# A graph transformer layer and a graph attention layer: context and layer 1 in another form, and the TensorE order laid down by hand

## The chip, the cores and the metric

The kernel runs on one core of a Trainium2 chip. The metric is the device time of one execution in microseconds; four to eight executions are taken of each kernel, and they agree within 0.3%. PE is TensorE, PEld its weight loads, DVE is VectorE, ACT is ScalarE and POOL is GpSimd in the lines of the profile. The "chain that ended last" is the chain of work followed back from the last instruction, at each step to what released it.

## The reference

There are 128 graphs ("batches") of 128 nodes with 512 features each, all in f32, and a weighted adjacency `adj` of 128x128 for each of them.

```python
# layer 0: pre-norm transformer, 8 heads of 64
h = relu(layernorm(x))
q, k, v = h @ Wq.T + bq, h @ Wk.T + bk, h @ Wv.T + bv      # split in heads
attn = softmax((q @ k.T) / 8 * (adj + adj))                # over the keys
x = x + (attn @ v) @ Wo.T + bo
# layer 1: graph attention
h = relu(layernorm(x))
Wh = h @ W
e = leaky_relu(Wh @ a[:512] + (Wh @ a[512:]).T, 0.2)
attention = softmax(where(adj > 0.5, e, -9e15), axis=1)    # over the rows
x = x + elu(attention @ Wh)
```

## The kernel before

Batches go in groups of four: the 512 rows of a group are the moving columns of the q and k projections. A framework writes the program: its scheduler decides the order of the instructions of each engine, from the order of the code and its own estimates. The parts that the change touches:

```python
def normed_T(dst, src, mv, rstd, b):
    """relu(layernorm(src)) with the features on the partitions."""
    hn = work.tile([P, E], F32, name="hn")
    nc.vector.tensor_scalar(hn, src, mv[:, b, 0:1], rstd[:, b : b + 1], op0=OP.subtract, op1=OP.mult)
    pt = ps1.tile([P, C, P], F32, name="pt", tag="ps1")
    for c in range(C):
        nc.tensor.transpose(pt[:, c, :], hn[:, c * P : (c + 1) * P], ident)
    nc.scalar.activation(dst, pt, AF.Relu)

def layer0_output(g, b, v, at, rs):
    # ... at is transposed into aT, head by head
    for j in range(H):
        head = 2 * (j % C) + j // C
        nc.tensor.matmul(pc[:, head, :], aT[:, j, :], v[:, head * D : (head + 1) * D], start=True, stop=True)
    nc.vector.tensor_tensor(cx, pc, rs[:, :, None].to_broadcast([P, H, D]), OP.mult)
    for c in range(C):
        nc.tensor.transpose(pt[:, c, :], cxf[:, c * P : (c + 1) * P], ident)
    nc.scalar.copy(cxT, pt)
    po = rows_matmul(cxT, wo_sb)
    # ... residual, statistics

def layer1_rows(g, b):
    normed_T(h2T, xs[g][:, b, :], mv1s[g], rstd, b)      # four transposes
    pw = rows_matmul(h2T, w1_sb)                         # project first, attend later
    # ...

# main loop, shortened
for g in range(NG + 1):
    layer0_qk(g)
    for b in range(G):
        scored = layer0_scores(g, b)
        if pending:
            layer0_output(*pending)
        pending = scored
        # ... layer 1 of group g - 1, the norm of group g + 1
```

## Time and profile before

| | before |
|---|---|
| time, median | 3728.24 us (3725.69 to 3730.71, four runs) |
| TensorE busy, share of the span | 90% |
| TensorE's share of the chain that ended last | 83% |
| mean granted TensorE clock | 0.964 |
| span per batch | 3721.6 / 128 = 29.07 us |

Four things are needed to read what follows. Each f32 matmul of the code stands in the trace as two matmul instructions, here called passes. In the groups of instructions a row is "line, engine, operation, output<-input, shapes, count | busy us, mean ns of one | idle time of the engine ahead of them and what ended it". TensorE's instructions overlap, so the mean of one is longer than the distance from one to the next: a 128x512 f32 pass reads 595 ns and follows its predecessor after 429 ns (3.43 us for eight). And the granted clock is what the throttle left of TensorE's full speed.

Two views of the kernel before are the group of the hn transposes (hn is the normed rows of a batch) and the timeline of TensorE around a context. The columns of the timeline are start, length, engine, line, operation, and in brackets the idle time before and who ended it.

```profile
L119 PE MATMUL pt<-ident,hn 128*128 128x128 f32 x1024 | 163.2, 278 | 85.0 <-DVE hn L116 85.0
```

```profile
1918.80 0.66 PE L210 MATMUL pt<-ident,cx 128*128 128x128 f32 x4 [0.79 <-DVE cx L206]
1920.13 5.40 PE L141 MATMUL pm<-wo,cxT 128*128 128x512 f32 x8 [0.68 <-ACT cxT L212]
```

TensorE waits for VectorE's scaled copy of the context, transposes it, waits for ScalarE's copy of the transposed context, and only then projects. The eight passes of the projection take 5.40 us here instead of 3.70, because the clock falls meanwhile: it is 1.00 up to 1920.8 and 0.50 from there to 1924.2. The change removes this sequence.

### The profile page before, as it was taken

Reading aid. Unit: us, or ns where it says so; the run is one execution under the profiler, and the core shown is the slowest. Engines: PE = TensorE matmul, PEld = TensorE weight load, DVE = VectorE, ACT = ScalarE, POOL = GpSimd, SP = SyncE. Lnnn points to the kernel's source line nnn. Section 1 sums busy time; section 2 is a strip of 40 time slices with the busy share of each in tenths; the row PEclk is TensorE's granted clock in tenths of the full one; section 3 lists DMA queues with packets and bytes.
Section 4 is the critical chain, followed back from the end, with each engine's and each line's share of the span. In section 5 each row is a group of like instructions: output and inputs, shape, how many; then the busy total and the mean of one; then the engine's idle time right before and its main releaser. Section 6 shows DMA issues by size and latency. Waiting matters only on the chain.

```text
span 3721.6 us, 32428 instructions
## 1 busy us (share of the span) xinstructions
PE 3335.5 (90%) x12416; PEld 1780.7 (48%) x12416; DVE 1620.8 (44%) x3008; ACT 975.1 (26%) x3201; POOL 260.3 (7%) x295
## 2 busy tenths in 40 slices
PE   7999889998889988999989899889998898998996
PEld 4444444454444444444444444444444544444443
DVE  3343443434444345444444443544444444445434
ACT  2222232222332223222223221232222222223221
POOL 1000000000000000000000000000000000000000
PEclk9999999999999999999999999999999999999998
DMA  3000000000000000000000000000000000000000
GB/s 110 1 26 26 26 3 23 26 26 26 4 26 23 26 26 15 15 23 26 26 18 12 23 26 26 26 3 26 23 26 26 4 26 23 26 26 8 18 12 23
DMA packets 55115, 83.87 MB, mean 23 GB/s; under 512 B 2736, under 2 KB 19120, under 8 KB 54960
## 3 DMA queue, kind: packets, MB, share of 16 engines
q1 hardware_dynamic: 50688, 75.50, 5.9%
q10 hardware_dynamic: 4272, 6.30, 0.5%
q8 instruction: 98, 1.61, 0.2%
q14 instruction: 57, 0.47, 0.0%
HBM read 48.24 MB, written 33.55 MB: 22 GB/s over the span
## 4 chain that ended last, share of the span: by engine, by line
PE 83%; DVE 8%; ACT 6%; issue 1%; POOL 1%; DMA 1%; ACTq 0%; POOLq 0%; DVEq 0%
PE pm L141 40%; PE pp L126 24%; PE pc L204 6%; PE sc L177 4%; PE pt L210 2%; DVE cx L206 2%; PE pt L119 2%; DVE at L179 2%; ACT h2T L120 2%; DVE st L110 2%; ACT cxT L212 2%; PE ph L269 1%; PE pa L196 1%; DVE x L214 1%; PE pb L240 1%
## 5 line engine op out<-in xcount | busy, mean ns | idle before, releaser
L141 PE MATMUL pm<-w,h2T 128*128 128x512 f32 x1024 | 525.3, 660 | 74.6 <-ACT h2T L120 74.6
L141 PE MATMUL pm<-wo,cxT 128*128 128x512 f32 x1024 | 524.2, 659 | 67.0 <-ACT cxT L212 67.0
L126 PE MATMUL pp<-hT,wq 128*128 128x512 f32 x1024 | 449.9, 597 | 42.8 <-ACT hT L120 42.8
L141 PE MATMUL pm<-wv,hT 128*128 128x512 f32 x1024 | 463.8, 595 | 0.2
L126 PE MATMUL pp<-hT,wk 128*128 128x512 f32 x1024 | 444.7, 592 | 0.0
L185 ACT ACTIVATE at<-at,nmx 128x128 f32<-128x128 f32 x1024 | 396.6, 389 | 118.3 <-DVE nmx L181 59.2
L141 PEld LDWEIGHTS pm<-w,h2T 128*128 128x128 f32 x1024 | 202.8, 208 | 318.3 <-issue 215.2
L141 PEld LDWEIGHTS pm<-wo,cxT 128*128 128x128 f32 x1024 | 201.5, 207 | 307.7 <-issue 213.7
L170 DVE TENSOR_TENSOR v<-pm,bv 128x512 f32<-128x512 f32 x128 | 88.2, 689 | 583.1 <-PE pm L141 583.1
L214 DVE TENSOR_TENSOR x<-pm,x 128x512 f32<-128x512 f32 x128 | 88.6, 692 | 551.1 <-PE pm L141 551.1
L126 PEld LDWEIGHTS pp<-hT,wq 128*128 128x128 f32 x1024 | 192.7, 191 | 281.3 <-issue 230.7
L126 PEld LDWEIGHTS pp<-hT,wk 128*128 128x128 f32 x1024 | 194.6, 190 | 244.9 <-issue 244.9
L136 ACT ACTIVATE kT<-pp,bk 128x512 f32<-128x512 f32 x128 | 88.0, 687 | 803.0 <-PE pp L126 803.0
L141 PEld LDWEIGHTS pm<-wv,hT 128*128 128x128 f32 x1024 | 187.0, 190 | 206.8 <-issue 199.2
L204 PEld LDWEIGHTS pc<-v,aT 128*128 128x128 f32 x2048 | 249.0, 192 | 54.6 <-issue 45.2
L204 PE MATMUL pc<-v,aT 128*128 128x64 f32 x2048 | 253.5, 274 | 0.8 <-DVE aT L198 0.7
L116 DVE TENSOR_SCALAR hn<-x,mv,rstd 128x512 f32<-128x512 f32 x256 | 136.8, 546 | 263.1 <-PE pt L119 203.9
L177 PE MATMUL sc<-kT,qT 64*128 64x128 f32 x2048 | 223.1, 303 | 18.5 <-DVE at L179 18.5
L119 PE MATMUL pt<-ident,hn 128*128 128x128 f32 x1024 | 163.2, 278 | 85.0 <-DVE hn L116 85.0
L133 DVE TENSOR_SCALAR qT<-pp,bq 128x512 f32<-128x512 f32 x128 | 96.1, 751 | 323.5 <-PE pp L126 323.5
L155 POOL TENSOR_TENSOR x<-x,bo 128x512 f32<-128x512 f32 x128 | 162.0, 1267 | 887.0 <-DVE hn L116 879.9
L119 PEld LDWEIGHTS pt<-ident,hn 128*128 128x128 f32 x1024 | 127.2, 143 | 194.4 <-DVE hn L116 92.2
(52 smaller groups left out, 3039.5 us busy)
## 6 DMA issues: line engine op xcount, KB each, us to landing
x<-in_x SPq DMA_DIRECT2D x32, 1024.0 KB, 5.3
out<-x SPq DMA_DIRECT2D x32, 1024.0 KB, 4.3
adj<-in_adj SPq DMA_DIRECT2D x32, 256.0 KB, 2.8
wq<-in_wqT ACTq DMA_DIRECT2D x1, 1024.0 KB, 8.3
wk<-in_wkT ACTq DMA_DIRECT2D x1, 1024.0 KB, 13.9
wv<-in_wvT ACTq DMA_DIRECT2D x1, 1024.0 KB, 13.2
wo<-in_woT ACTq DMA_DIRECT2D x1, 1024.0 KB, 10.6
w<-in_w ACTq DMA_DIRECT2D x1, 1024.0 KB, 12.5
```

The costliest lines, as they stand in the source:

```text
L116: nc.vector.tensor_scalar(hn, src, mv[:, b, 0:1], rstd[:, b : b + 1], op0=OP.subtract, op1=OP.mult)
L119: nc.tensor.transpose(pt[:, c, :], hn[:, c * P : (c + 1) * P], ident)
L126: nc.tensor.matmul(pp, w[:, c, f * P : (f + 1) * P], hT[:, c].rearrange("p b s -> p (b s)"), start=(c == 0), stop=(c == C - 1),)
L133: nc.vector.tensor_scalar(dst, pp, bq_sb[:, f : f + 1], QSCALE, op0=OP.add, op1=OP.mult)
L136: nc.scalar.activation(dst, pp, AF.Identity, bias=bk_sb[:, f : f + 1])
L141: nc.tensor.matmul(pm, lhsT[:, c, :], w[:, c, :], start=(c == 0), stop=(c == C - 1))
L155: nc.gpsimd.tensor_tensor(xs[g][:, b, :], xs[g][:, b, :], bo_sb, OP.add)
L170: nc.vector.tensor_tensor(v, pv, bv_sb, OP.add)
L177: nc.tensor.matmul(sc[:, s * C + i, :], qT[r, i, cols], kT[r, i, cols], start=True, stop=True)
L185: nc.scalar.activation(at[:, j, :], at[:, j, :], AF.Exp, bias=nmx[:, j : j + 1], accum_out=sums[:, head : head + 1])
L204: nc.tensor.matmul(pc[:, head, :], aT[:, j, :], v[:, head * D : (head + 1) * D], start=True, stop=True)
L214: nc.vector.tensor_tensor(xg[:, b, :], po, xg[:, b, :], OP.add)
```

## The change

The intent, as far as the code shows it, has five parts.

- The context is made already transposed, as v^T x attention^T, two heads side by side in the two halves of the output partitions. Four transposes and one of two copies go. The attention must then be scaled by its row sums ahead of its transpose, and GpSimd does it.
- Layer 1 applies the attention to the normed rows, then projects. Its four transposes go, and so does the transpose of the adjacency, which is loaded transposed.
- Constants are folded (the bias of v into that of the output, the two vectors of layer 1 into W).
- The pipeline is one of single batches: in step t, batch t is scored, t-1 projected, t-2 finished in layer 1, t+8 normed.
- TensorE's order is taken from the code and not from the scheduler.

```diff
+    def context(b):
+        pc = ps1.tile([P, C, S], F32, name="pc", tag="ps1")
+        for i in range(C):
+            for s in range(2):
+                head = 2 * i + s
+                nc.tensor.matmul(
+                    pc[s * D : (s + 1) * D, i, :], vs[b][:, head * D : (head + 1) * D], ats[b][:, s * C + i, :],
+                    start=True, stop=True,
+                )
+        cxs[b] = work.tile([P, C, S], F32, name="cxT")
+        nc.scalar.copy(cxs[b], pc)
...
+    def hidden(b):
+        mv = row_stats(xs[b])
+        rstd = rstd_of(mv)
+        hn = work.tile([P, E], F32, name="hn")
+        nc.vector.tensor_scalar(hn, xs[b], mv[:, 0:1], rstd, op0=OP.subtract, op1=OP.mult)
+        pt = ps1.tile([P, C, P], F32, name="pt", tag="ps1")
+        for c in range(C):
+            nc.tensor.transpose(pt[:, c, :], hn[:, c * P : (c + 1) * P], ident)
+        nc.scalar.activation(hTs[g][:, :, i, :], pt, AF.Relu)
...
+        nc.gpsimd.tensor_tensor(at, at, rs[:, :, None].to_broadcast([P, H, S]), OP.mult)   # in scores(b)
...
+        nc.vector.tensor_scalar(neg, adjTs[b], 0.5, NEG_INF, op0=OP.is_le, op1=OP.mult)    # in output0(b)
...
+    def gather1(b):
+        for c in range(C):
+            nc.tensor.matmul(pg[:, c, :], h2[:, c * P : (c + 1) * P], w, start=True, stop=True)
+        nc.scalar.copy(gT, pg)
...
+    with tc.manual_schedule(engines={PE}):
+        for t in range(B + 3):                       # the guards on t are left out here
+            load_x(t + 2 * G); load_adj(t + 2)
+            scores(t)
+            qk_unit(g + 1, 2 * i)
+            attention1(t - 2)
+            output0(t - 1)
+            hidden(t + 2 * G)
+            values(t)
+            gather1(t - 2)
+            qk_unit(g + 1, 2 * i + 1)
+            attn_T(t)
+            output1(t - 2)
+            context(t)
```

More of the change, by code (lines that the diff above doesn't have):

```diff
@@ L9 @@
 F32 = mybir.dt.float32
-U8 = mybir.dt.uint8
 AF = mybir.ActivationFunctionType
@@ L13 @@
 AX = mybir.AxisListType
+PE = mybir.EngineType.PE
 P = 128
@@ L29 @@
     adj: bass.AP,
+    adjT: bass.AP,
     wqT: bass.AP,
@@ L44, with load_x, load_adj @@
     C = E // P
-    NG = B // G
     QSCALE = 2.0 / D**0.5
     const = ctx.enter_context(tc.tile_pool(name="const", bufs=1))
-    io = ctx.enter_context(tc.tile_pool(name="io", bufs=3))
+    io = ctx.enter_context(tc.tile_pool(name="io", bufs=15))
+    aio = ctx.enter_context(tc.tile_pool(name="aio", bufs=6))
     grp = ctx.enter_context(tc.tile_pool(name="grp", bufs=2))
     work = ctx.enter_context(tc.tile_pool(name="work", bufs=2))
-    small = ctx.enter_context(tc.tile_pool(name="small", bufs=4))
+    small = ctx.enter_context(tc.tile_pool(name="small", bufs=6))
     ps1 = ctx.enter_context(tc.tile_pool(name="ps1", bufs=4, space=bass.MemoryType.PSUM))
     ps2 = ctx.enter_context(tc.tile_pool(name="ps2", bufs=2, space=bass.MemoryType.PSUM))
-    xs, adjs = {}, {}
-    def load(g):
-        rows = slice(g * G, (g + 1) * G)
-        xs[g] = io.tile([P, G, E], F32, name="x")
-        nc.sync.dma_start(xs[g], x[rows].rearrange("b s e -> s b e"))
-        adjs[g] = io.tile([P, G, S], F32, name="adj")
-        nc.sync.dma_start(adjs[g], adj[rows].rearrange("b s t -> s b t"))
-    load(0)
+    xs, adjs, adjTs = {}, {}, {}
+    def load_x(b):
+        xs[b] = io.tile([P, E], F32, name="x")
+        nc.sync.dma_start(xs[b], x[b])
+    def load_adj(b):
+        adjs[b] = aio.tile([P, S], F32, name="adj")
+        nc.sync.dma_start(adjs[b], adj[b])
+        adjTs[b] = aio.tile([P, S], F32, name="adjT")
+        nc.sync.dma_start(adjTs[b], adjT[b])
+    for b in range(2 * G):
+        load_x(b)
     ident = const.tile([P, P], F32, name="ident")
     make_identity(nc, ident)
-    mhalf = const.tile([P, G], F32, name="mhalf")
+    mhalf = const.tile([P, 1], F32, name="mhalf")
     nc.gpsimd.memset(mhalf, -0.5)
@@ L93, with row_stats @@
     wv_sb = weight(wvT, "wv")
-    bv_sb = row(bv, 0, "bv")
     wo_sb = weight(woT, "wo")
-    bo_sb = row(bo, 0, "bo")
+    bv_sb = column(bv, "bv")
+    c_sb = row(bo, 0, "c")
     w1_sb = weight(w1, "w1")
-    as_sb = row(a1, 0, "a_src")
-    at_sb = row(a1, E, "a_dst")
+    us_sb = row(a1, 0, "u_src")
+    ut_sb = row(a1, E, "u_dst")
+    for b in range(2):
+        load_adj(b)
     def rstd_of(mv):
-        r = small.tile([P, G], F32, name="rstd")
-        nc.gpsimd.tensor_scalar_add(r, mv[:, :, 1], EPS)
+        r = small.tile([P, 1], F32, name="rstd")
+        nc.gpsimd.tensor_scalar_add(r, mv[:, 1:2], EPS)
         nc.gpsimd.tensor_tensor(r, r, mhalf, OP.pow)
         return r
-    def row_stats(mv, b, src):
+    def row_stats(src):
         st = small.tile([P, nc.vector.BN_STATS_DIM], F32, name="st")
         nc.vector.bn_stats(st, src)
-        nc.vector.bn_aggr(mv[:, b, :], st)
-    def normed_T(dst, src, mv, rstd, b):
-        hn = work.tile([P, E], F32, name="hn")
-        nc.vector.tensor_scalar(hn, src, mv[:, b, 0:1], rstd[:, b : b + 1], op0=OP.subtract, op1=OP.mult)
-        pt = ps1.tile([P, C, P], F32, name="pt", tag="ps1")
-        for c in range(C):
-            nc.tensor.transpose(pt[:, c, :], hn[:, c * P : (c + 1) * P], ident)
-        nc.scalar.activation(dst, pt, AF.Relu)
-    def project(dst, w, hT, finish):
-        for f in range(C):
-            pp = ps1.tile([P, G * S], F32, name="pp", tag="ps1")
-            for c in range(C):
-                nc.tensor.matmul(
-                    pp, w[:, c, f * P : (f + 1) * P], hT[:, c].rearrange("p b s -> p (b s)"),
-                    start=(c == 0), stop=(c == C - 1),
-                )
-            finish(dst[:, f], pp, f)
-    def finish_q(dst, pp, f):
-        nc.vector.tensor_scalar(dst, pp, bq_sb[:, f : f + 1], QSCALE, op0=OP.add, op1=OP.mult)
-    def finish_k(dst, pp, f):
-        nc.scalar.activation(dst, pp, AF.Identity, bias=bk_sb[:, f : f + 1])
+        mv = small.tile([P, 2], F32, name="mv")
+        nc.vector.bn_aggr(mv, st)
+        return mv
     def rows_matmul(lhsT, w):
@@ L142, in rows_matmul @@
         return pm
-    hTs, qks, mv1s, l1s = {}, {}, {}, {}
-    def layer0_norm(g, b):
-        if b == 0:
-            mv = small.tile([P, G, 2], F32, name="mv")
-            for i in range(G):
-                row_stats(mv, i, xs[g][:, i, :])
-            hTs[g] = grp.tile([P, C, G, S], F32, name="hT"), mv, rstd_of(mv)
-        hT, mv, rstd = hTs[g]
-        normed_T(hT[:, :, b, :], xs[g][:, b, :], mv, rstd, b)
-        nc.gpsimd.tensor_tensor(xs[g][:, b, :], xs[g][:, b, :], bo_sb, OP.add)
-    def layer0_qk(g):
-        hT = hTs[g][0]
-        qT = grp.tile([P, C, G * S], F32, name="qT")
-        kT = grp.tile([P, C, G * S], F32, name="kT")
-        project(qT, wq_sb, hT, finish_q)
-        project(kT, wk_sb, hT, finish_k)
-        qks[g] = qT, kT
@@ L165, in layer0_scores @@
-    def layer0_scores(g, b):
-        ag, hT, (qT, kT) = adjs[g], hTs[g][0], qks[g]
-        cols = slice(b * S, (b + 1) * S)
-        pv = rows_matmul(hT[:, :, b, :], wv_sb)
-        v = work.tile([P, E], F32, name="v")
-        nc.vector.tensor_tensor(v, pv, bv_sb, OP.add)
+    hTs, qks, ats, vs, cxs, l1s = {}, {}, {}, {}, {}, {}
+    def hidden(b):
+        g, i = divmod(b, G)
+        if i == 0:
+            hTs[g] = grp.tile([P, C, G, S], F32, name="hT", bufs=3)
+        mv = row_stats(xs[b])
[6 more added lines that the diff above has]
+        nc.scalar.activation(hTs[g][:, :, i, :], pt, AF.Relu)
@@ new lines, in qk_unit @@
+    def qk_unit(g, n):
+        f, is_k = divmod(n, 2)
+        if n == 0:
+            qks[g] = grp.tile([P, C, G * S], F32, name="qT"), grp.tile([P, C, G * S], F32, name="kT")
+        w = wk_sb if is_k else wq_sb
+        dst = qks[g][is_k][:, f]
+        pp = ps1.tile([P, G * S], F32, name="pp", tag="ps1")
+        for c in range(C):
+            nc.tensor.matmul(
+                pp, w[:, c, f * P : (f + 1) * P], hTs[g][:, c].rearrange("p b s -> p (b s)"),
+                start=(c == 0), stop=(c == C - 1),
+            )
+        if is_k:
+            nc.scalar.activation(dst, pp, AF.Identity, bias=bk_sb[:, f : f + 1])
+        else:
+            nc.vector.tensor_scalar(dst, pp, bq_sb[:, f : f + 1], QSCALE, op0=OP.add, op1=OP.mult)
@@ L173, in layer0_scores, with values, scores @@
+    def values(b):
+        g, i = divmod(b, G)
+        pv = rows_matmul(hTs[g][:, :, i, :], wv_sb)
+        vs[b] = work.tile([P, E], F32, name="v")
+        nc.vector.tensor_copy(vs[b], pv)
+    def scores(b):
+        g, i = divmod(b, G)
+        qT, kT = qks[g]
+        cols = slice(i * S, (i + 1) * S)
         sc = ps2.tile([P, H, S], F32, name="sc", tag="ps2")
@@ L177, in layer0_scores @@
                 nc.tensor.matmul(sc[:, s * C + i, :], qT[r, i, cols], kT[r, i, cols], start=True, stop=True)
-        at = work.tile([P, H, S], F32, name="at")
-        nc.vector.tensor_tensor(at, sc, ag[:, b, None, :].to_broadcast([P, H, S]), OP.mult)
+        at = work.tile([P, H, S], F32, name="at", bufs=3)
+        nc.vector.tensor_tensor(at, sc, adjs[b][:, None, :].to_broadcast([P, H, S]), OP.mult)
         nmx = small.tile([P, H], F32, name="nmx")
@@ L183, in layer0_scores, with attn_T @@
         for j in range(H):
-            head = 2 * (j % C) + j // C
-            nc.scalar.activation(
-                at[:, j, :], at[:, j, :], AF.Exp, bias=nmx[:, j : j + 1], accum_out=sums[:, head : head + 1]
-            )
+            nc.scalar.activation(at[:, j, :], at[:, j, :], AF.Exp, bias=nmx[:, j : j + 1], accum_out=sums[:, j : j + 1])
         rs = small.tile([P, H], F32, name="rs")
         nc.vector.reciprocal(rs, sums)
-        return g, b, v, at, rs
-    def layer0_output(g, b, v, at, rs):
-        xg = xs[g]
+        nc.gpsimd.tensor_tensor(at, at, rs[:, :, None].to_broadcast([P, H, S]), OP.mult)
+        ats[b] = at
+        nc.gpsimd.tensor_tensor(xs[b], xs[b], c_sb, OP.add)
+    def attn_T(b):
         pa = ps2.tile([P, H, S], F32, name="pa", tag="ps2")
         for j in range(H):
-            nc.tensor.transpose(pa[:, j, :], at[:, j, :], ident)
+            nc.tensor.transpose(pa[:, j, :], ats[b][:, j, :], ident)
         aT = work.tile([P, H, S], F32, name="aT")
@@ L199, in layer0_output @@
         nc.scalar.copy(aT[:, C:], pa[:, C:])
-        pc = ps1.tile([P, H, D], F32, name="pc", tag="ps1")
-        for j in range(H):
-            head = 2 * (j % C) + j // C
-            nc.tensor.matmul(pc[:, head, :], aT[:, j, :], v[:, head * D : (head + 1) * D], start=True, stop=True)
-        cx = work.tile([P, H, D], F32, name="cx")
-        nc.vector.tensor_tensor(cx, pc, rs[:, :, None].to_broadcast([P, H, D]), OP.mult)
-        cxf = cx.rearrange("p h d -> p (h d)")
-        pt = ps1.tile([P, C, P], F32, name="pt", tag="ps1")
@@ L209, in layer0_output @@
-        for c in range(C):
-            nc.tensor.transpose(pt[:, c, :], cxf[:, c * P : (c + 1) * P], ident)
-        cxT = work.tile([P, C, P], F32, name="cxT")
-        nc.scalar.copy(cxT, pt)
-        po = rows_matmul(cxT, wo_sb)
-        nc.vector.tensor_tensor(xg[:, b, :], po, xg[:, b, :], OP.add)
-        if b == 0:
-            mv1s[g] = small.tile([P, G, 2], F32, name="mv1")
-        row_stats(mv1s[g], b, xg[:, b, :])
-    def layer1_rows(g, b):
-        if b == 0:
-            wh = grp.tile([P, G, E], F32, name="wh")
-            wsum = small.tile([P, 2, G], F32, name="wsum")
-            l1s[g] = wh, wsum, rstd_of(mv1s[g])
-        wh, wsum, rstd = l1s[g]
-        h2T = work.tile([P, C, P], F32, name="h2T")
-        normed_T(h2T, xs[g][:, b, :], mv1s[g], rstd, b)
-        pw = rows_matmul(h2T, w1_sb)
-        nc.scalar.copy(wh[:, b, :], pw)
-        junk = work.tile([P, E], F32, name="junk", bufs=1)
-        for i, a in ((0, as_sb), (1, at_sb)):
-            nc.vector.scalar_tensor_tensor(
-                junk, pw, 1.0, a, op0=OP.mult, op1=OP.mult, accum_out=wsum[:, i, b : b + 1]
-            )
@@ L235, in layer1_attention @@
-    def layer1_attention(g):
-        ag, (wh, wsum, _) = adjs[g], l1s[g]
-        pb = ps1.tile([P, G, S], F32, name="pb", tag="ps1")
-        for b in range(G):
-            nc.tensor.matmul(
-                pb[:, b, :], wsum[:, 0, b : b + 1].to_broadcast([P, P]), ident, start=True, stop=True
-            )
-        e = work.tile([P, G, S], F32, name="e")
-        nc.vector.tensor_tensor(e, pb, wsum[:, 1, :, None].to_broadcast([P, G, S]), OP.add)
-        nc.vector.scalar_tensor_tensor(e, e, ALPHA, e, op0=OP.mult, op1=OP.max)
-        pj = ps1.tile([P, G, S], F32, name="pj", tag="ps1")
-        for b in range(G):
-            nc.tensor.transpose(pj[:, b, :], ag[:, b, :], ident)
-        edge = work.tile([P, G, S], U8, name="edge")
-        nc.vector.tensor_scalar(edge, pj, 0.5, None, op0=OP.is_gt)
-        w = work.tile([P, G, S], F32, name="w")
-        nc.gpsimd.memset(w, NEG_INF)
-        nc.vector.copy_predicated(w, edge, e)
-        nmx = small.tile([P, G], F32, name="nmx1")
-        nc.vector.tensor_reduce(nmx, w, AX.X, OP.max, negate=True)
-        sums = small.tile([P, G], F32, name="sums1")
-        for b in range(G):
-            nc.scalar.activation(
-                w[:, b, :], w[:, b, :], AF.Exp, bias=nmx[:, b : b + 1], accum_out=sums[:, b : b + 1]
-            )
-        rs = small.tile([P, G], F32, name="rs1")
-        nc.vector.reciprocal(rs, sums)
-        l1s[g] = wh, w, rs
@@ L265, in layer1_output @@
-    def layer1_output(g, b):
-        xg, (wh, w, rs) = xs[g], l1s[g]
-        nc.vector.tensor_scalar_mul(w[:, b, :], w[:, b, :], rs[:, b : b + 1])
-        ph = ps1.tile([P, E], F32, name="ph", tag="ps1")
-        nc.tensor.matmul(ph, w[:, b, :], wh[:, b, :], start=True, stop=True)
-        ez = work.tile([P, E], F32, name="ez")
-        nc.vector.tensor_scalar_min(ez, ph, 0.0)
-        nc.scalar.activation(ez, ez, AF.Exp)
-        nc.vector.scalar_tensor_tensor(xg[:, b, :], ph, 0.0, xg[:, b, :], op0=OP.max, op1=OP.add)
-        nc.vector.scalar_tensor_tensor(xg[:, b, :], ez, -1.0, xg[:, b, :], op0=OP.add, op1=OP.add)
-        if b == G - 1:
-            nc.sync.dma_start(out[g * G : (g + 1) * G].rearrange("b s e -> s b e"), xg)
@@ L281 @@
-    for b in range(G):
-        layer0_norm(0, b)
-    pending = None
-    for g in range(NG + 1):
-        if g + 1 < NG:
-            load(g + 1)
-        if g < NG:
-            layer0_qk(g)
-        for b in range(G):
-            scored = layer0_scores(g, b) if g < NG else None
-            if pending:
-                layer0_output(*pending)
-            pending = scored
-            if g:
-                if b < 2:
-                    layer1_rows(g - 1, 2 * b)
-                    layer1_rows(g - 1, 2 * b + 1)
-                if b == 1:
-                    layer1_attention(g - 1)
-                if b >= 2:
-                    layer1_output(g - 1, 2 * b - 4)
-                    layer1_output(g - 1, 2 * b - 3)
-            if g + 1 < NG:
-                layer0_norm(g + 1, b)
+        ats[b] = aT
@@ new lines, in context, with output0 @@
+    def context(b):
[3 more added lines that the diff above has]
+                head = 2 * i + s
+                nc.tensor.matmul(
+                    pc[s * D : (s + 1) * D, i, :], vs[b][:, head * D : (head + 1) * D], ats[b][:, s * C + i, :],
+                    start=True, stop=True,
+                )
+        cxs[b] = work.tile([P, C, S], F32, name="cxT")
+        nc.scalar.copy(cxs[b], pc)
+    def output0(b):
+        po = rows_matmul(cxs[b], wo_sb)
+        nc.vector.tensor_tensor(xs[b], po, xs[b], OP.add)
+        mv = row_stats(xs[b])
+        rstd = rstd_of(mv)
+        h2 = work.tile([P, E], F32, name="h2", bufs=4)
+        nc.vector.tensor_scalar(h2, xs[b], mv[:, 0:1], 0.0, op0=OP.subtract, op1=OP.max)
+        ws = small.tile([P, 2], F32, name="ws")
+        junk = work.tile([P, E], F32, name="junk", bufs=1)
+        for i, u in ((0, us_sb), (1, ut_sb)):
+            nc.vector.scalar_tensor_tensor(
+                junk, h2, 1.0, u, op0=OP.mult, op1=OP.mult, accum_out=ws[:, i : i + 1]
+            )
+        nc.gpsimd.tensor_tensor(ws, ws, rstd.to_broadcast([P, 2]), OP.mult)
+        neg = work.tile([P, S], F32, name="neg")
+        nc.vector.tensor_scalar(neg, adjTs[b], 0.5, NEG_INF, op0=OP.is_le, op1=OP.mult)
+        l1s[b] = h2, ws, rstd, neg
@@ new lines, in attention1 @@
+    def attention1(b):
+        h2, ws, rstd, neg = l1s[b]
+        pb = ps1.tile([P, S], F32, name="pb", tag="ps1")
+        nc.tensor.transpose(pb, ws[:, 0:1].to_broadcast([P, P]), ident)
+        w = work.tile([P, S], F32, name="w", bufs=3)
+        nc.scalar.activation(w, pb, AF.Prelu, bias=ws[:, 1:2], alpha=ALPHA)
+        nc.vector.tensor_tensor(w, w, neg, OP.add)
+        nmx = small.tile([P, 1], F32, name="nmx1")
+        nc.vector.tensor_reduce(nmx, w, AX.X, OP.max, negate=True)
+        sums = small.tile([P, 1], F32, name="sums1")
+        nc.scalar.activation(w, w, AF.Exp, bias=nmx, accum_out=sums)
+        rs = small.tile([P, 1], F32, name="rs1")
+        nc.vector.reciprocal(rs, sums)
+        nc.vector.tensor_scalar(w, w, rs, rstd, op0=OP.mult, op1=OP.mult)
+        l1s[b] = h2, w
@@ new lines, in gather1, with output1 @@
+    def gather1(b):
+        h2, w = l1s[b]
+        pg = ps1.tile([P, C, S], F32, name="pg", tag="ps1")
+        for c in range(C):
+            nc.tensor.matmul(pg[:, c, :], h2[:, c * P : (c + 1) * P], w, start=True, stop=True)
+        gT = work.tile([P, C, S], F32, name="gT")
+        nc.scalar.copy(gT, pg)
+        l1s[b] = gT
+    def output1(b):
+        pw = rows_matmul(l1s[b], w1_sb)
+        ez = work.tile([P, E], F32, name="ez")
+        nc.scalar.activation(ez, pw, AF.Exp)
+        nc.vector.scalar_tensor_tensor(xs[b], pw, 0.0, xs[b], op0=OP.max, op1=OP.add)
+        nc.vector.scalar_tensor_tensor(xs[b], ez, 1.0, xs[b], op0=OP.min, op1=OP.add)
+        nc.sync.dma_start(out[b], xs[b])
@@ new lines, in constants @@
+    def constants():
+        pm = ps1.tile([P, E], F32, name="pm", tag="ps1")
+        for c in range(C):
+            nc.tensor.matmul(
+                pm, bv_sb[:, c : c + 1].to_broadcast([P, P]), wo_sb[:, c, :], start=(c == 0), stop=(c == C - 1)
+            )
+        nc.vector.scalar_tensor_tensor(c_sb, pm, -1.0, c_sb, op0=OP.add, op1=OP.add)
+        ucol = const.tile([P, 2, C], F32, name="ucol")
+        junk = work.tile([P, E], F32, name="junk", bufs=1)
+        for i, u in ((0, us_sb), (1, ut_sb)):
+            for c in range(C):
+                nc.vector.scalar_tensor_tensor(
+                    junk, w1_sb[:, c, :], 1.0, u, op0=OP.mult, op1=OP.mult, accum_out=ucol[:, i, c : c + 1]
+                )
+        for i, u in ((0, us_sb), (1, ut_sb)):
+            pu = ps1.tile([P, C, P], F32, name="pu", tag="ps1")
+            for c in range(C):
+                nc.tensor.transpose(pu[:, c, :], ucol[:, i, c : c + 1].to_broadcast([P, P]), ident)
+            nc.scalar.copy(u, pu.rearrange("p c k -> p (c k)"))
@@ new lines @@
+    with tc.manual_schedule(engines={PE}):
+        for b in range(G):
+            hidden(b)
+        for n in range(2 * C):
+            qk_unit(0, n)
+            if n % 2:
+                hidden(G + n // 2)
+        constants()
+        for t in range(B + 3):
+            g, i = divmod(t, G)
+            if t + 2 * G < B:
+                load_x(t + 2 * G)
+            if t + 2 < B:
+                load_adj(t + 2)
+            if t < B:
+                scores(t)
+            if (g + 1) * G < B:
+                qk_unit(g + 1, 2 * i)
+            if 0 <= t - 2 < B:
+                attention1(t - 2)
+            if 0 <= t - 1 < B:
+                output0(t - 1)
+            if t + 2 * G < B:
+                hidden(t + 2 * G)
+            if t < B:
+                values(t)
+            if 0 <= t - 2 < B:
+                gather1(t - 2)
+            if (g + 1) * G < B:
+                qk_unit(g + 1, 2 * i + 1)
+            if t < B:
+                attn_T(t)
+            if 0 <= t - 2 < B:
+                output1(t - 2)
+            if t < B:
+                context(t)
@@ L316 @@
         "adj": adj,
+        "adjT": np.transpose(adj, (0, 2, 1)),
         "wqT": np.transpose(L0_gnn_Wq),
```

## The prediction

> **What bounds the kernel now.** I read the busy table first, then the chain of waits, then the groups by line. The first two (times in us; the chain gives shares of the span):
>
> ```profile
> PE 3335.5 (90%) x12416; PEld 1780.7 (48%) x12416; DVE 1620.8 (44%) x3008; ACT 975.1 (26%) x3201; POOL 260.3 (7%) x295
> PE 83%; DVE 8%; ACT 6%; issue 1%; POOL 1%; DMA 1%; ACTq 0%; POOLq 0%; DVEq 0%
> ...
> L141 PE MATMUL pm<-w,h2T 128*128 128x512 f32 x1024 | 525.3, 660 | 74.6 <-ACT h2T L120 74.6
> L141 PE MATMUL pm<-wo,cxT 128*128 128x512 f32 x1024 | 524.2, 659 | 67.0 <-ACT cxT L212 67.0
> ...
> L141 PE MATMUL pm<-wv,hT 128*128 128x512 f32 x1024 | 463.8, 595 | 0.2
> ```
>
> TensorE carries the end: 83% of the chain. The last three rows do the same work, but two of them wait for a copy by ScalarE and take 64 ns more each: the clock, below. Span 3722 over 128 batches is 29.07 us a batch. From the timeline, eight 128x512 f32 passes (four matmuls) follow each other in 3.43 us, a 128x128 pass in 0.107, sixteen score passes in 1.1, sixteen context passes in 1.72. So TensorE at full pace needs per batch, in us: q, k, v, output and layer 1 5 x 3.43 = 17.15; scores 1.1; attention transposes 0.86; context 1.72; three sets of four transposes 1.3; layer 1's gather 0.86; row sums and adjacency transpose 0.3: 23.3. The other 5.8 us are waits and a slow clock.
>
> The clock: in the timeline of the drain (columns: start, length, engine, line, operation), eight passes take 3.70 with their latency at full pace, and this after pauses:
>
> ```profile
> 3676.74 1.12 PE L119 MATMUL pt<-ident,hn 128*128 128x128 f32 x4 [3.75 <-DVE hn L116]
> 3678.54 5.45 PE L141 MATMUL pm<-w,h2T 128*128 128x512 f32 x8 [0.69 <-ACT h2T L120]
> 3683.83 0.60 PE L119 MATMUL pt<-ident,hn 128*128 128x128 f32 x4
> 3685.17 3.70 PE L141 MATMUL pm<-w,h2T 128*128 128x512 f32 x8 [0.74 <-ACT h2T L120]
> ```
>
> After 3.75 us idle the transposes cost 0.5 more and the matmuls 1.75 more. The view by windows gives a granted clock of 0.50 there.
>
> The third reading concerns the port that VectorE and GpSimd share:
>
> ```profile
> 1913.67 1.27 POOL L155 TENSOR_TENSOR x<-x,bo 128x512 f32<-128x512 f32 x1 [5.61 <-DVE hn L116]
> 1914.22 1.26 DVE L245 SCALAR_TENSOR_TENSOR e<-e 128x512 f32<-128x512 f32 x1
> ...
> L245 DVE SCALAR_TENSOR_TENSOR e<-e x32: 691/1260/1261, 190.9 to 3702.0; 128x512 f32<-128x512 f32 x32
> ```
>
> L245 takes two inputs from SBUF. It takes 691 ns alone, and 1260 whenever GpSimd's add runs: it does its work after that add has ended.
>
> **What the Trainium skill says.** "SBUF — State Buffer", Who interferes with whom: a VectorE instruction with two SBUF inputs, or in a two-port mode (which f32 tensor_scalar in SBUF can enter), and a GpSimd instruction that reads SBUF exclude each other, the later one blocking fully. L245 agrees (691 against 1260). "TensorE: Matmul & The Clock Gate", What's actually happening: an idle window of some 3.4 us halves the clock, a busy one restores it; the trace agrees (0.50 after 3.75 us). The same page, Architectural detail: VectorE and ScalarE run strictly in order, and TensorE's matmuls too. I compared VectorE's order in the built program with the trace between 1000 and 1500 us: identical over 580 instructions. "TensorEngine Tiling (Array Packing)", Performance Considerations: outputs of 64 columns allow two column tiles side by side; no column tile is in this trace, but the scores, tiled by rows, do 16 passes in 1.1 us instead of 1.72.
>
> **The change, part by part**, per batch.
>
> TensorE loses the transposes of the context (0.43), of layer 1's rows (0.43) and of the adjacency (0.11; it is now loaded transposed); the row sums halve (0.1); the context as two column tiles should take some 1.1 instead of 1.72 (estimate, the scores' pace). Layer 1's gather stays at 0.86 (eight passes of 128 columns). Sum: 23.3 - 1.7 = 21.6 us of dense TensorE; 128 x 21.6 plus some 60 us of start would be about 2850 us. VectorE's work is about 12 us, ScalarE's 8, GpSimd's 6, the extra 8 MB of DMA nothing at 23 GB/s: no engine's sum is the bound. GpSimd newly scales the attention before its transpose: 128x1024, by the add's 1.267 us per 512 about 2.53 us.
>
> But TensorE's order is now fixed. Per batch: scores, q part, layer-1 row, output projection, transposes of hn (the normed rows of the batch eight ahead), v, gather, k part, attention transposes, layer-1 projection, context. I read the built program's VectorE order and the instruction behind each wait. VectorE's order is: mask, maximum, q, reciprocal, layer-1 mask add, its maximum, neg, reciprocal, residual, scaling, two row statistics and aggregates, h2, **then hn**. Thus hn, whose input has long been there, stands behind everything that needs this batch's exponentials. I walk it from the end of the scores (0), with durations of the rows of before:
>
> - mask 1.22, maximum 1.21 (to 2.52); eight exponentials 3.19 (timeline: 0.385 apart; to 5.74); reciprocal 0.2 (5.97).
> - GpSimd's scaling 6.05 to 8.58. In that time VectorE comes to the layer-1 mask add (two SBUF inputs) and to neg (tensor_scalar in SBUF): at least one blocks until about 8.5, by L245's pattern.
> - Then add, maximum, exponential, reciprocal about 1.2 (9.75; some 0.7 less if the mask add gets in first); residual 0.69, scaling 0.28, two statistics 1.3, aggregates 0.25, overlapping by 0.08 each (12.0).
> - GpSimd: two rstd, of which hn needs the second: 2 x (0.23 + power) + gaps 0.24. The power takes 1.04 for four columns; for one, between 0.43 (estimate: most of it per column) and 1.04. hn 0.55. TensorE can start hn's transposes at 13.6 to 15.5, say 14.5.
>
> TensorE itself is there at 3.43 + 0.11 + 3.43 = 7.0. It stands still for about 7.5 us in each batch. From hn's transposes to the next scores' end: 0.44 + 3.43 + 0.87 + 3.43 + 0.86 + 3.43 + 1.1 + 1.16 = 14.7. The idle halves the clock: 0.45 on the transposes and about 1.7 on v, 2.1 in all. So 14.5 + 14.7 + 2.1 = **31.3 us a batch against 29.07**. 120 batches have an hn; start, the last eight without it, and drain are some 60 + 165 + 40 = 265 us (estimate: 22 us for four of them, 19 for the last four). 120 x 31.3 + 265 = 4020 us.
>
> **The rivals.**
>
> First, TensorE stays dense: about 2850 us, if hn were early enough. For it: its input is loaded eight batches ahead and the order was made with that purpose. Against it: VectorE's built order, in which hn follows three serial trips between VectorE and ScalarE or GpSimd.
>
> Second, the order is as I say but the sizes are small: no blocking at the shared port and a short power. Then hn's transposes start near 11.8, a batch is 11.8 + 14.7 + 2.1 = 28.6, and the time 120 x 28.6 + 265 = 3700: the same as before. Without the clock loss too, 26.5 and 3445. Against it: neg would meet GpSimd's scaling even if the mask add slips in first. For it: the blocking of tensor_scalar rests on the page and on nine instances of hn in the trace that overlap the add's last 0.3 us and take 0.58 instead of 0.55 us; that is thin.
>
> Third, GpSimd's 3-d broadcast scaling takes longer than twice the add, say 3.5 us: everything after it moves by a further microsecond, 32.3 us and 4140.
>
> **Range and chances.** The walk gives 4020 with 28.6 to 32.3 us a batch. I shade it to 3940, since small misses of the chain (power, blocking, clock) mostly lie below the middle I took. The range is 3680, the second rival, to 4160, the third. Faster by 2% needs less than 3652, 28.2 us a batch: 0.14, mostly for a mistake about the order. Within 2% (to 3801): 0.17. Slower: 0.69.
>
> **What would show it.** The groups of after should have a wait of 5 to 8 us per batch (120 of them, 600 to 900 us in all) before the hn transposes on TensorE, with hn on VectorE as releaser, and nothing comparable elsewhere on TensorE; a granted clock well below the 0.964 of before; neg or the mask add with a duration of 1 to 2.6 us instead of 0.3; GpSimd's scaling near 2.5 us; the one-column power between 0.43 and 1.04; context passes in 1.0 to 1.2 us per batch; the chain of waits with TensorE at 60% or less and VectorE, ScalarE and GpSimd sharing the rest. The prediction is wrong if hn runs while ScalarE does the exponentials, if TensorE's busy share stays near 90% or rises, or if the clock does not drop in pauses of this length.

## The result, and the profile after

The changed kernel takes 3920.25 us (3918.11 to 3921.19, four runs) against 3728.24 us: it is slower, by a ratio of 1.0514 (95% interval 1.0500 to 1.0529).

The busy row, the chain of waits by engine and four groups of the changed kernel:

```profile
PE 3151.0 (80%) x11920; PEld 1623.5 (41%) x11920; DVE 1759.5 (45%) x3089; ACT 970.4 (25%) x3203; POOL 722.3 (18%) x903
PE 58%; DVE 21%; ACT 11%; POOL 6%; issue 4%; DMA 1%; POOLq 0%; SPq 0%; ACTq 0%; DVEq 0%
L126 PE MATMUL pm<-wv,hT 128*128 128x512 f32 x1024 | 733.3, 884 | 0.0
L142 PE MATMUL pt<-ident,hn 128*128 128x128 f32 x512 | 136.4, 421 | 730.5 <-DVE hn L139 730.5
L126 PE MATMUL pm<-w,gT 128*128 128x512 f32 x1024 | 463.0, 595 | 1.6 <-ACT gT L259 1.5
L126 PE MATMUL pm<-wo,cxT 128*128 128x512 f32 x1024 | 460.7, 593 | 0.5 <-ACT cxT L214 0.5
```

The output and layer-1 projections, which waited 67 and 75 us in all before, now hardly wait (0.5 and 1.6 us) and run at full pace (593 and 595 ns). What the change was made for has come. In its place there is one large wait: 730.5 us ahead of the transposes of hn, ended by VectorE's hn (85.0 us before, for the transposes of both layers). The work right behind it is slow: a v pass reads 884 ns, a transpose 421 instead of 278. TensorE is down from 83% to 58% of the chain, and the mean granted clock from 0.964 to 0.895.

Now one batch in the timeline of all engines, from the last exponentials on:

```profile
1902.47 0.20 DVE L187 RECIPROCAL rs<-sums 128x8 f32<-128x8 f32 x1 [1.36 <-ACT at L185]
1902.72 0.29 DVE L242 TENSOR_TENSOR w<-w,neg 128x128 f32<-128x128 f32 x1
1902.82 1.95 POOL L188 TENSOR_TENSOR at<-at,rs 128x1024 f32<-128x1024 f32 x1 [21.27 <-DVE rs L187]
1903.05 0.29 DVE L244 TENSOR_REDUCE nmx<-w 128x1 f32<-128x128 f32 x1
1903.25 1.60 DVE L232 TENSOR_SCALAR neg<-adjT 128x128 f32<-128x128 f32 x1
...
1904.78 0.15 DVE L248 RECIPROCAL rs<-sums 128x1 f32<-128x1 f32 x1
...
1905.69 1.27 DVE L118 BATCH_NORM_STATS2 st<-x 128x6 f32<-128x512 f32 x2
...
1908.57 0.57 POOL L113 TENSOR_TENSOR rstd<-rstd,mhalf 128x1 f32<-128x1 f32 x1
1909.18 0.55 DVE L139 TENSOR_SCALAR hn<-x,mv,rstd 128x512 f32<-128x512 f32 x1 [1.61 <-POOL rstd L113]
...
1909.87 1.09 PE L142 MATMUL pt<-ident,hn 128*128 128x128 f32 x4 [6.00 <-DVE hn L139]
```

VectorE starts the reciprocal (L187) only when ScalarE is done with the exponentials, and hn (L139) comes 6.7 us later, at the end of the row of instructions that the prediction listed. TensorE has been idle for 6.00 us by then. In between, neg (L232) takes 1.60 us and ends within 0.1 us of GpSimd's scaling (1902.82 + 1.95 = 1904.77); alone it takes 0.21, the shortest of the 128 instances. The same reciprocal stands at 1933.20 in the next batch, so a batch takes 30.73 us.

### The profile page after: what moved, and what is told of

It is laid out like the page before. It is cut to its first block, busy times and chain, and to the rows that moved or that the text cites. A ratio compares the mean times of both kernels' runs of the same rounds, so it can differ in the third digit from the quotient of the medians. Undisturbed runs are those within 1.5% of the kernel's fastest.

```text
span 3919.4 us, 33353 instructions
## 1 busy us (share of the span) xinstructions
PE 3151.0 (80%) x11920; PEld 1623.5 (41%) x11920; DVE 1759.5 (45%) x3089; ACT 970.4 (25%) x3203; POOL 722.3 (18%) x903
## 3 DMA queue, kind: packets, MB, share of 16 engines
q8 instruction: 94, 1.54, 0.2%
## 4 chain that ended last, share of the span: by engine, by line
PE 58%; DVE 21%; ACT 11%; POOL 6%; issue 4%; DMA 1%; POOLq 0%; SPq 0%; ACTq 0%; DVEq 0%
PE pm L126 30%; PE pp L154 12%; ACT at L185 10%; DVE at L180 4%; DVE nmx L182 4%; DVE st L118 4%; PE sc L178 4%; POOL rstd L113 3%; PE pt L142 3%; PE pc L209 3%; PE pg L257 3%; PE pa L197 3%; POOL rstd L112 2%; DVE neg L232 2%; DVE x L218 2%
## 5 line engine op out<-in xcount | busy, mean ns | idle before, releaser
L126 PE MATMUL pm<-wv,hT 128*128 128x512 f32 x1024 | 733.3, 884 | 0.0
L188 POOL TENSOR_TENSOR at<-at,rs 128x1024 f32<-128x1024 f32 x128 | 250.1, 1954 | 2581.7 <-DVE rs L187 2560.1
L142 PE MATMUL pt<-ident,hn 128*128 128x128 f32 x512 | 136.4, 421 | 730.5 <-DVE hn L139 730.5
L126 PE MATMUL pm<-w,gT 128*128 128x512 f32 x1024 | 463.0, 595 | 1.6 <-ACT gT L259 1.5
L126 PEld LDWEIGHTS pm<-wv,hT 128*128 128x128 f32 x1024 | 300.4, 307 | 357.4 <-issue 356.4
L199 DVE COPY aT<-pa 128x512 f32<-128x512 f32 x128 | 88.6, 692 | 560.1 <-PE pa L197 560.1
L267 DVE SCALAR_TENSOR_TENSOR x<-pm,x 128x512 f32<-128x512 f32 x128 | 88.6, 692 | 444.8 <-ACT ez L266 444.8
L126 PEld LDWEIGHTS pm<-w,gT 128*128 128x128 f32 x1024 | 185.4, 191 | 187.1 <-issue 184.5
L192 POOL TENSOR_TENSOR x<-x,c 128x512 f32<-128x512 f32 x128 | 206.6, 1617 | 128.6 <-DVE hn L139 78.6
L227 DVE SCALAR_TENSOR_TENSOR junk<-h,u_dst 128x512 f32<-128x512 f32 x128 | 200.0, 1563 | 4.3
L232 DVE TENSOR_SCALAR neg<-adjT 128x128 f32<-128x128 f32 x128 | 196.6, 1536 | 2.0 <-DMA adjT<-in_adjT 2.0
```

Of the source, the lines that this page charges most:

```text
L126: nc.tensor.matmul(pm, lhsT[:, c, :], w[:, c, :], start=(c == 0), stop=(c == C - 1))
L188: nc.gpsimd.tensor_tensor(at, at, rs[:, :, None].to_broadcast([P, H, S]), OP.mult)
L192: nc.gpsimd.tensor_tensor(xs[b], xs[b], c_sb, OP.add)
L227: nc.vector.scalar_tensor_tensor(junk, h2, 1.0, u, op0=OP.mult, op1=OP.mult, accum_out=ws[:, i : i + 1])
L232: nc.vector.tensor_scalar(neg, adjTs[b], 0.5, NEG_INF, op0=OP.is_le, op1=OP.mult)
```

## The experiments

All eight kernels gave correct results. They ran in two calls of four, with medians of the kernel before at 3724.11 and 3723.70 us. The theory was that hn's place in VectorE's queue makes TensorE, whose order is fixed, wait in each batch, and that the clock falls in the pause. The rivals were the new work itself (GpSimd's scaling and its hold on the shared port, small transfers) and a low clock of another origin.

### hn one batch earlier

```diff
-        mv = row_stats(xs[b]); rstd = rstd_of(mv); hn = ...       # inside hidden(b)
+    def hidden_norm(b):                                           # statistics, rstd and hn, bufs=3
...
             scores(t)
+            hidden_norm(t + 2 * G + 1)                            # x is also loaded a batch earlier
...
             hidden(t + 2 * G)                                     # now only the transposes and the copy
```

> The only edit: hn (statistics, rstd and normalising of a batch's rows) is issued one batch earlier than its transposes, with a third hn buffer. Theory A (hn stands in VectorE's in-order queue behind this batch's exponentials, and TensorE, whose order is fixed, waits for it; the clock falls in the pause): the 730 us wait before the hn transposes goes to under 60 us, the granted clock goes to 0.98 or more, TensorE runs at about 21.8 us a batch (its passes in the trace of the changed kernel: 3.54+0.11+3.45+0.44+3.43+0.89+3.44+0.87+3.53+1.02+1.09), and the time is about 2880 us (2820 to 3000). Rival B (the new work itself, GpSimd's scaling and its hold on the port shared with VectorE, sets the pace): the time stays above 3700. Rival C (the clock is low for another reason than this pause): the wait goes, the clock stays near 0.90 and the time is 3100 to 3250.

Measured: 2868.45 us (2868.09 to 2868.92), a ratio of 0.7702 to the kernel before (0.7691 to 0.7714). The busy row, the chain and the two groups that were slow:

```profile
PE 2809.8 (98%) x11920; PEld 1485.0 (52%) x11920; DVE 1746.9 (61%) x3089; ACT 970.8 (34%) x3203; POOL 722.7 (25%) x903
PE 97%; DMA 1%; DVE 1%; POOL 1%; ACT 0%; issue 0%; ACTq 0%; DVEq 0%
L126 PE MATMUL pm<-wv,hT 128*128 128x512 f32 x1024 | 460.7, 593 | 0.0
L149 PE MATMUL pt<-ident,hn 128*128 128x128 f32 x512 | 78.1, 277 | 15.1 <-DVE hn L137 15.1
```

The wait has gone but for 15.1 us at the start, the v passes and transposes are back at 593 and 277 ns, the clock is 0.997, and TensorE carries 97% of the chain. From the scores of one batch to those of the next it is 21.80 us in the timeline. The same instructions run on each engine, and VectorE's built order per batch is the same as in the changed kernel: hn is still behind neg and the rest, and neg still takes 1.54 us. Only the batch that hn belongs to has changed, with a third buffer for hn and an earlier load of x to allow it. So nothing in the new work is too slow by itself; this one wait and its clock cost 3920 - 2868 = 1052 us.

### hn in its own batch, but ahead in VectorE's queue

The first experiment gives hn a whole batch of time. To test the place in the queue itself, this one keeps hn in the batch in which it is transposed, and lays down VectorE's order too.

```diff
             scores(t)                          # mask, maximum, exponentials
+            hidden_norm(t + 2 * G)             # statistics, rstd, hn
             qk_unit(g + 1, 2 * i)
+            scale(t)                           # reciprocal, GpSimd's scaling: was in scores
...
-    with tc.manual_schedule(engines={PE}):
+    with tc.manual_schedule(engines={PE, mybir.EngineType.DVE}):
```

> No batch of lead: hn is made in the batch in which it is transposed, as in the changed kernel, but VectorE's order is laid down too, with the statistics, aggregate and hn right after the maximum, ahead of the reciprocal that waits for the exponentials. Theory A in its exact form (the place in VectorE's queue, not the length of hn's own chain): hn is ready about 2.5 + 0.68 + 0.17 + 0.9 (rstd on GpSimd) + 0.55 = 5 us after the scores, before TensorE arrives at 7.0; the wait goes to under 60 us and the time is 2870 (2840 to 3000). If hn's own chain, or a lead of a batch, is what matters: 3300 or more.

Measured: 2869.23 us (2868.52 to 2870.00), ratio 0.7703 (0.7691 to 0.7716). VectorE's timeline there:

```profile
1908.26 1.22 DVE L189 TENSOR_REDUCE nmx<-at 128x8 f32<-128x1024 f32 x1
1909.39 0.69 DVE L118 BATCH_NORM_STATS2 st<-x 128x6 f32<-128x512 f32 x1
1910.11 0.18 DVE L120 BATCH_NORM_AGGREGATE mv<-st 128x2 f32<-128x6 f32 x1
1911.29 0.55 DVE L137 TENSOR_SCALAR hn<-x,mv,rstd 128x512 f32<-128x512 f32 x1 [1.00 <-POOL rstd L113]
...
1912.73 0.20 DVE L198 RECIPROCAL rs<-sums 128x8 f32<-128x8 f32 x1 [0.23 <-ACT at L192]
```

hn is done at 1911.84, before the reciprocal that waits for the exponentials, and it needs 2.5 us from the start of its statistics. In the changed kernel it fell behind waits for other work. TensorE's wait for hn is 11.2 us in all here, in four places.

This edit moves more than hn: VectorE's whole order is now that of the code, so neg comes later and takes 0.22 us, and GpSimd adds the bias before it scales. The first experiment has neither of these, and this one has neither the third buffer nor the earlier load. What the two share is that hn is ready before TensorE comes to its transposes. What neg alone is worth, the next experiment measures.

### neg on GpSimd

```diff
-        nc.vector.tensor_scalar(neg, adjTs[b], 0.5, NEG_INF, op0=OP.is_le, op1=OP.mult)
+        nc.gpsimd.tensor_scalar(neg, adjTs[b], 0.5, NEG_INF, op0=OP.is_le, op1=OP.mult)
```

> The only edit: the mask of layer 1 (neg) is computed by GpSimd, in order after its scaling of the attention, so that VectorE does not meet GpSimd at the shared port (neg took 1.54 us there, 0.28 expected alone). Theory A with blocking as a term of the chain: hn comes 0.9 us earlier per batch (the exponential of layer 1 ends at 3.87 in the trace window, the reciprocal could only start at 4.78), TensorE's wait falls from 6.0 to about 5.1 us, the time by 120 x 0.9 = 110 us to about 3810. If the blocking was beside the chain: 3920, unchanged. If the blocking were the main cause (rival B): below 3700.

Measured: 3743.40 us (3741.94 to 3745.57), ratio to before 1.0052 (1.0036 to 1.0069). It is 177 us faster than the changed kernel, where 110 had been expected. The group that the wait stands in, and the timeline:

```profile
L142 PE MATMUL pt<-ident,hn 128*128 128x128 f32 x512 | 136.2, 421 | 627.8 <-DVE hn L139 627.8
```

```profile
1902.65 0.29 DVE L244 TENSOR_REDUCE nmx<-w 128x1 f32<-128x128 f32 x1
1903.49 0.16 DVE L248 RECIPROCAL rs<-sums 128x1 f32<-128x1 f32 x1 [0.56 <-ACT w L246]
...
1908.60 1.09 PE L142 MATMUL pt<-ident,hn 128*128 128x128 f32 x4 [5.14 <-DVE hn L139]
1909.48 4.51 PE L126 MATMUL pm<-wv,hT 128*128 128x512 f32 x8
```

The wait fell from 6.00 to 5.14 us, and from 730.5 to 627.8 in all: 103 us, as expected from the 0.9. The remaining 74 us are about what the v passes give (733.3 us busy in the changed kernel, 654.4 here). The trace's record of the granted clock shows why: in the changed kernel the clock stands at 0.50 for 6.83 us in each of 120 batches (1908.57 to 1915.40 is one such stretch), and here for 6.83 us 66 times and for 3.41 us 55 times. The expectation had left that out. Blocking at the shared port is therefore a real term of the chain, but a small one beside the place of hn.

### Dead matmuls in the pause

```diff
+    def warm():   # nobody reads pd
+        pd = ps1.tile([P, E], F32, name="pd", tag="ps1")
+        for c in range(6):
+            nc.tensor.matmul(pd, wv_sb[:, c % C, :P], wq_sb[:, c % C, :], start=(c == 0), stop=(c == 5))
...
+                warm()
                 hidden(t + 2 * G)
```

> The order and the wait are kept; six dead matmuls (12 passes of 512 columns, 5.15 us) fill the pause of 6 us ahead of the hn transposes, nobody reads them. Theory A with the clock as a term: the clock stays up (over 0.97), the hn transposes take 0.6 instead of 1.09 us and v 3.6 instead of 5.9, and the time falls by 120 x 2.3 = 280 us to about 3640, although TensorE does more work. If the pause does not set the clock: no gain, 3920 or more. If TensorE were the bound and not the wait: plus 5.15 us a batch, over 4400.

Measured: 3592.46 us (3592.29 to 3593.92), ratio to before 0.9647 (0.9632 to 0.9661); about 3640 had been expected. With 5.15 us more work per batch for TensorE the kernel is 328 us faster than the changed one. The timeline:

```profile
1907.55 5.31 PE L275 MATMUL pd<-wq,wv 128*128 128x512 f32 x12
1913.62 0.66 PE L142 MATMUL pt<-ident,hn 128*128 128x128 f32 x4 [0.76 <-DVE hn L139]
1914.12 3.60 PE L126 MATMUL pm<-wv,hT 128*128 128x512 f32 x8
```

The clock is 0.999, and v takes 3.60 us where it took 5.91. This measures the clock as a term by itself: 328 / 120 = 2.73 us per batch.

That figure belongs to this length of batch and is not the price of any pause. In the middle of the run a batch takes 27.93 us in the mean with the clock held up, and 30.72 (30.66 to 30.84) in the changed kernel. The stretches at 0.50 come in steps of 3.41 us, and 30.72 is nine steps of 3.413. So it looks as if the changed kernel's batch is drawn to a whole number of steps; no run here tests that.

The experiment also shows that TensorE's work was not the bound. It is a measurement and no remedy, since taking the pause away brings the time to 2868 us.

### TensorE's order, fixed and free

Two kernels leave the order to the scheduler again, one with the changed kernel's hn and one with hn a batch earlier.

```diff
-    with tc.manual_schedule(engines={PE}):
+    if True:
```

> The same operations without the fixed TensorE order: the scheduler orders TensorE as it does in the kernel before. In its built order the attention transposes and the next scores come ahead of the hn transposes, and hn ahead of the next mask on VectorE. Theory A (the fixed order together with hn's place is what costs, not the operations): faster than before, about 3450 (3200 to 3650), since the residual, statistics, rstd and hn are still some 5 us after the output projection and only 2 us of other work lie in between. Rival (the new operations are the cost): 3850 or more.

> The batch of lead for hn, with TensorE's order left to the scheduler. Its built order is nearly that of the fixed one. If the fixed order was only harmful with hn late, and not itself a gain: 2870 (2840 to 2900), as with the fixed order. If the fixed order is worth something by itself: over 2930.

| | hn in the batch, where the code has it | hn one batch earlier |
|---|---|---|
| TensorE's order fixed | 3920.25 us (the changed kernel) | 2868.45 us |
| TensorE's order free | 3516.48 us (3512.67 to 3518.09) | 2868.01 us (2864.01 to 2869.95) |

The kernel with the free order and late hn misses its central 3450 but lies in the range that was given. Its TensorE does other work first and still waits:

```profile
1919.11 1.09 PE L197 MATMUL pa<-ident,at 128*128 128x128 f32 x8 [1.51 <-POOL at L188]
1920.14 1.16 PE L178 MATMUL sc<-kT,qT 64*128 64x128 f32 x16
1923.55 1.12 PE L142 MATMUL pt<-ident,hn 128*128 128x128 f32 x4 [2.26 <-DVE hn L139]
1924.46 4.62 PE L126 MATMUL pm<-wv,hT 128*128 128x512 f32 x8
```

Over the run it waits 399 us for hn and 46 us for GpSimd's scaling, at a clock of 0.939. So the fixed order is worth -404 us with hn late, and nothing (0.4 us, inside the scatter) with hn early. The gain over the kernel before does not come from laying down the order by hand: with hn early the scheduler finds the same one (the timelines of TensorE between 1900 and 1940 us have the same sequence). Whether another order would do as well was not tried.

### Both remedies together

This is the first experiment's kernel with neg on GpSimd.

> Lead for hn and neg on GpSimd together. The blocked neg (1.54 us on VectorE) is then on no path that TensorE waits for, since TensorE is at 98% of the span: no change against the lead alone, 2868 within 10 us. If the port still costs something at the end: about 2760.

Measured: 2868.47 us (2867.61 to 2869.47). The blocked neg, worth 177 us while it stood on the chain, is worth nothing beside a TensorE that never waits.

### The context as before

```diff
-                nc.tensor.matmul(pc[s * D : (s + 1) * D, i, :], vs[b][:, head * D : (head + 1) * D], ats[b][:, s * C + i, :], ...)
+            nc.tensor.matmul(pc[:, head, :], ats[b][:, j, :], vs[b][:, head * D : (head + 1) * D], ...)
+        cxs[b] = ...; nc.scalar.copy(cxs[b], pc)
+    def context_T(b):      # placed after the next batch's scores
+        for c in range(C):
+            nc.tensor.transpose(pt[:, c, :], cxs[b][:, c * P : (c + 1) * P], ident)
+        nc.scalar.copy(cxs[b], pt)
```

> Lead for hn, but the context as in the kernel before: attention x v with 64 moving columns, copied, transposed in four pieces, copied again; the transposes stand after the next scores so that TensorE does not wait for the copies. TensorE's sum grows by 1.72 - 1.02 = 0.70 us (context passes) and 0.44 us (transposes) a batch: 2868 + 128 x 1.14 = 3015 (2990 to 3060). If the new form of the context is worth no more than its transposes: 2925. If the copies come back as waits: over 3100.

Measured: 3008.27 us (3007.46 to 3010.25), 140 us above the same kernel with the new context. The scores follow the context's start by 1.82 us here (1922.11 to 1923.93) and by 1.03 in the first experiment (1920.53 to 1921.56); the first line is of the old form, the second of the new:

```profile
1922.11 1.89 PE L215 MATMUL pc<-v,aT 128*128 128x64 f32 x16
```

```profile
1920.53 1.09 PE L216 MATMUL pc<-aT,v 128*64 128x128 f32 x16
```

Column tiles bring 0.79 us a batch and the four transposes 0.50 (1925.02 to 1925.52 in the same timeline), 1.29 together. Part of it is given back in two projections: from the start of layer 1's projection to the context's start it is 3.53 us with the new form (1917.00 to 1920.53 in the first experiment) and 3.44 with the old (1918.67 to 1922.11), and the q part after the scores takes 3.54 (1900.85 to 1904.39) against 3.43 (1902.62 to 1906.05, where the context's transposes stand between). 1.29 - 0.09 - 0.11 = 1.09 us, which is the measured 140 / 128 = 1.09. What makes those projections longer was not isolated. The new context is a gain that the changed kernel's wait had covered up.

The other parts of the change were not taken back one by one. Of the 29.07 - 21.80 = 7.27 us a batch between the kernel before and the first experiment's, about 1.5 are less work for TensorE (the prediction's 23.3 less 21.80), and the rest are waits and slow passes of the kernel before.

## Why the prediction was right

The prediction named 3940 us and a slower kernel; 3920.25 was measured. Its steps, by its own terms:

- **TensorE would be dense without the wait, at 21.6 us a batch and about 2850 us.** The kernels with hn early show 21.80 us and 2868 us. (The prediction's own terms, 128 x 21.6 + 60, make 2825 and not 2850.) The estimate of the column tiles (1.1 us) was close to the 1.02 measured.
- **hn stands behind this batch's exponentials.** The built order said so and the trace shows it. Two experiments that take hn out of this place, in two ways, bring 2868 and 2869 us.
- **hn's transposes would start 13.6 to 15.5 us after the scores, say 14.5.** They started 13.2 after (scores' end 1927.41 in the timeline, less 30.73, to 1909.87), a little below the stated range. Two terms were too large: GpSimd's scaling took 1.95 us and not 2.53, and the mask add got in first (0.29 us at 1902.72, just ahead of GpSimd), which the prediction had named as possible and had priced at 0.7. One was too small: GpSimd's first rstd add took 0.51 us instead of 0.23. The power was 0.57 for one column, inside the range given.
- **One VectorE instruction blocks at the shared port until GpSimd ends.** It was neg, with 1.54 us in the mean. The experiment with neg on GpSimd shows its effect on the time. The two-port case of tensor_scalar, called thin evidence, holds: "SBUF — State Buffer", Who interferes with whom, has it, and also the other direction, seen here in that rstd add of 0.51 instead of 0.22 us while VectorE's h2 ran. The prediction's "after that add has ended" is a shade too strict: L245 ends 0.55 us after the add, though alone it takes 0.69, and neg ends 0.08 us after the scaling, though alone it takes 0.21.
- **The clock costs 2.1 us a batch.** Measured by itself it was 2.73. This term was too small and the one above too large, by 0.6 and 1.3. That the sum of 31.3 us a batch came near 30.73 is luck in part, since the two errors have opposite signs. Start, tail and the last eight batches were 3919 - 120 x 30.73 = 232 us, not 265.
- **The shading from 4020 to 3940** was a judgement on the terms as a whole, and no single run tests it. The walk itself missed by 101 us: 68 by the batch (120 x 0.57) and 33 by start and tail. That 3940 lies nearer is owed to the shading, whose reason held for the power and the blocking but not for the clock.

The prediction's rivals: a TensorE that stays dense (2850) was wrong for this kernel and right for each kernel with hn early. The second, no blocking and a short power (3700), was half right: the power was short, but neg blocked, as the prediction had argued against it; with the blocking taken away by hand the time is 3743 us. The third, a scaling of 3.5 us, is refuted by the 1.95 measured. Of the experiments' rivals, blocking as the main cause is refuted by the kernel with neg on GpSimd, the new operations as a cost by the first experiment.

## What to carry to other kernels

When the order of one engine is laid down by hand, read the built order of the engines that feed it: an instruction whose input has long been there can stand behind one that waits, and then the fixed engine waits for both. Work out such a wait by walking the chain from a fixed point with measured durations, and add what the clock costs after the pause. Give what feeds the bound engine a stage of lead in the pipeline, or a place ahead of the wait; either brought this kernel from 3920 us to 2868 or 2869, 23% below the kernel before.

## What the Trainium skill lacked or had wrong

- "TensorE: Matmul & The Clock Gate", What's actually happening: it speaks of idle windows of some 3.4 us. In the kernel before, two pauses of 0.7 to 0.9 us on either side of four transposes were already followed by slow passes of the output projection in 21 batches (5.40 us for eight instead of 3.70 in the one shown), and by passes at full pace in 42 others. The page gives no length for pauses as short as these.
- The same page does not say that the period of a loop may settle on the clock's steps. Here a batch took 30.72 us, nine times 3.413, where 27.93 was enough with the clock held up; the figures suggest it, and no run tests it.
- "GPSIMD Engine Reference" has no figure for a power: 1.04 us for 128x4 and 0.57 for 128x1. A multiplication of 128x1024 with a broadcast second operand took 1.95 us, less than twice the 1.27 of an addition of 128x512 with two full ones.
- "TensorEngine Tiling (Array Packing)", Theoretical Speedup, gives up to 2x for a dimension of 64 and no measured figure: sixteen f32 passes took 1.03 us against 1.82, 1.77 times as fast, with the moving side 128 columns wide instead of 64.
